# The maxima of a chunk by one product, a third buffer for halves of q and k, and moved slots in an AdaLN block

## The chip, the cores and the metric

The kernel runs on one core of a Trainium2 chip. The metric is the time of one execution in microseconds (us); lower is better. A core has TensorE (PE: matrix products, with its weight loads PEld), VectorE (DVE), ScalarE (ACT), GpSimd (POOL) and SyncE (SP), which here issues nearly all DMA transfers. All data is float32.

## The reference

An AdaLN block: modulated layer norm, causal attention with 16 heads of 16, and a gated feed-forward network with a mix of neighbouring tokens. There are 8 batches of 1024 tokens of 256 numbers. Cut to what is computed:

```python
mod = (silu(c) @ wmod).reshape(8, 6, 1, -1)
sa, ca, ga, sb, cb, gb = (mod[:, 0], ..., mod[:, 5])
ga = (2 * (ga >= 0) - 1) * maximum(abs(ga), 0.25)      # gb in the same way
h = layernorm(x) * (1 + ca) + sa
q, k, v = split(einsum('bnd,ed->bne', h, w_in), 3)      # each as 16 heads of 16
scores = einsum('bhqd,bhkd->bhqk', q, k) * 16 ** -0.5   # causal: -inf above the diagonal
out = softmax(scores) @ v
x = x + ga * (out @ w_out.T + b_out)
h = layernorm(x) * (1 + cb) + sb
xr, xk = mu * h + (1 - mu) * h_prev                     # with mu_r and mu_k
x = x + gb * sigmoid(xr @ W_r.T) * (square(relu(xk @ W_k.T)) @ W_v.T)
```

## The kernel before

**Units and chunks.** A batch has two chunks of 512 tokens (c = 0, 1). Attention is cut into 32 units u: four heads of one batch. A unit's q and k lie on the chip as 128 partitions: four strips of 32 rows, one for each head, of which 16 hold the head's numbers. Row 16 of a strip of q holds the negated maximum of each query, and that of k holds ones, so that the second product of the scores comes out with its maximum subtracted.

**Two passes over the scores.** The first pass ("S") makes scores with queries on the partitions (`pp`, by `maxima`), and VectorE takes their maxima into a small tile `max`; the second ("T") makes them again with keys on the partitions (`pw`, by `weights`), ScalarE takes the exponential into `w`, POOL clears what lies above the diagonal, and `attend` multiplies with v into `po`. A pass goes through a unit in nine pieces: a to e touch the diagonal, 0 to 3 are whole. When all maxima of a chunk are there, `join` (for chunk 1) and, a step later, `subtract` run: products with the identity turn the maxima (`pmx`), ScalarE negates them (`mrow`), and a transfer (`q<-mrow`) writes them into row 16 of the strips of q.

**The loop.** `step` runs once for each number `now`: one piece of T for one unit, one piece of S for a unit that is 9 steps (`LAG`) ahead, both in two halves of two heads, products of both halves first; then what is due in `soon` (subtract among it), then the slot's list `fill`, and last `finish`, which calls `attend` where a group of pieces ends. TensorE, and from the loop on every engine, takes its instructions in the order in which the program gives them (`InOrder`). A function handed to `later` issues its transfer at the start of a later step, urgent ones first; SyncE works through them in order and waits for each one's data.

**Banks.** PSUM has four one-bank buffers with tag "t" (`pw` of the four heads, `pmx`, `po` and all products of the fill, in turn) and two of two banks with tag "s" (`pp`, a half each).

**Slots.** The tables `POST`, `PREP`, `PREP_FIRST`, `START` and others say in which step a piece of other work stands; an entry is a step and a name, entries of one step run in the order of the table. `START` and `compact` count from step 0, the others from step 9 + 36 b, b being the batch whose second pass begins there: this stretch is called a stage below. In `POST` (stages 1 to 6), x and y are the two chunks of the batch before: project (a product py, added to x by VectorE), stats, norm, turn, mix and mixed (VectorE; mixed0 into `mix`, mixed1 into `step`), receptance, key, value (a product pkv, multiplied with r by VectorE, added by POOL). In `PREP` (stages 1 to 6) and `PREP_FIRST` (stage 0), m and n are the two chunks of the next batch: stats, norm, turn (transposes into hT), q0, k0, q1, k1 (a product pq of half the heads, copied by ScalarE to a buffer `qk`, and written to DRAM a step later as `pad<-qk`, from where q and k of a unit are read) and v0, v2 (a product pv, copied to v). `START` does it for batch 0, beside `direct`, which makes q and k of the first units without DRAM; `compact` packs the weights of q and k, which the products pq need.

**Gates.** `gates` runs in step 17: a product, two copies of ScalarE, five operations of POOL, and a transfer of the gates to DRAM.

Every engine instruction is recorded by one helper, so all rows of the profile name its line, L123; they are told apart by their tiles. Instructions of one tile for pieces a to e carry the piece in the name (`pp_a`, `w_a`), whole ones don't.

Of the kernel before, what the change touches and what calls it, by code (L numbers as in the profile page):

```python
# [8 lines left out]
F32 = mybir.dt.float32  # L9
# [5 lines left out]
P = 128  # L15
# [3 lines left out]
CW = 512  # L19
NC = N // CW  # L20
NT = CW // P
HG = 4
# [7 lines left out]
KEPT = 4  # L30
# [42 lines left out]
def adaln_block(  # L73
# [72 lines left out]
    def later(f, steps=1, urgent=False):  # L146

        if strict[0]:
            due.append((clock[0] + steps, not urgent, f))
        else:  # L150
            f()
# [82 lines left out]
    q_of, k_of = [], []  # L234
# [43 lines left out]
    def row_of(t):  # L278

        return strips(t)[:, HD, :]  # L280
# [30 lines left out]
    def gates():  # L311

        pg = bank("pg")
        for c in range(DC):
            pe.matmul(
                pg[:B, :],
                scT[:, c, :],
                wgate[:, c].rearrange("p n e -> p (n e)"),
                start=(c == 0),
                stop=(c == DC - 1),  # L320
            )
        both = sb.tile([B, 2, 2 * D], F32, tag="h", bufs=2, name="gates")
        sign, gate = both[:, 0, :], both[:, 1, :]
        act.activation(gate, pg[:B, :], AF.Abs)
        act.copy(sign, pg[:B, :])
        pool.tensor_scalar(sign, sign, 0.0, 2.0, ALU.is_ge, ALU.mult)
        pool.tensor_scalar_max(gate, gate, 0.25)
        pool.tensor_scalar_add(sign, sign, -1.0)
        pool.tensor_mul(gate, gate, sign)
        pool.tensor_scalar_mul(gate[:, D:], gate[:, D:], 0.5)  # L330
        later(lambda: sync.dma_start(gates_of, gate))

    def rows_of_gates(b):

# [81 lines left out]
    def prep(b, c):  # L416
        S = A[b, c]

        def stats(half):
            statistics(S["xa"], S, f"a{b}_{c}", half)  # L420

        def norm(half):
            normalise(S["xa"], S, f"a{b}_{c}", half)
            if half == 0:
                return
            nxt = b * NC + c + 1
            if 1 < nxt < B * NC:
                later(lambda: load_xa(nxt // NC, nxt % NC))

        def turn():  # L430
            S["hT"] = sb.tile([P, DC, CW], F32, tag="hT", bufs=2, name=f"hT{b}_{c}")
            for d in range(DC):
                name = f"pta{b}_{c}_{d}"
                transposed(S["h"], S["hT"][:, d, :], b, d, SHIFT_A, SCALE_A, name)

        def qk(n, half):

            pq = bank(f"pq{b}_{c}_{n}_{half}")
            at = n * D + half * P
            for d in range(DC):  # L440
                pe.matmul(
                    pq,
                    wqk_sb[:, d, at : at + P],
                    S["hT"][:, d, :],
                    start=(d == 0),
                    stop=(d == DC - 1),
                )
            w = sb.tile([P, CW], F32, tag="qk", bufs=2, name=f"qk{b}_{c}_{n}_{half}")
            if n == 0:
                act.mul(w, pq, SCALE)  # L450
            else:
                act.copy(w, pq)

            later(lambda: sync.dma_start(padded_of[b % 2][n][half][c, :, :HD, :], w))

        def v(t0):
            pv = bank(f"pv{b}_{c}_{t0}")
            rows(pv, S["hT"], wv_sb, (t0, t0 + 1))
            to = v_of[(b * NC + c) % (2 * NC)]
            act.copy(  # L460
                to[:, t0 : t0 + 2, : H * (HD + 1)].rearrange(
                    "p t (h e) -> p t h e", e=HD + 1
                )[:, :, :, :HD],
                pv.rearrange("p (t h e) -> p t h e", t=2, e=HD),
            )

        return dict(
            stats0=lambda: stats(0),
            stats1=lambda: stats(1),
            norm0=lambda: norm(0),  # L470
            norm1=lambda: norm(1),
            turn=turn,
            q0=lambda: qk(0, 0),
            k0=lambda: qk(1, 0),
            q1=lambda: qk(0, 1),
            k1=lambda: qk(1, 1),
            v0=lambda: v(0),
            v2=lambda: v(2),
        )
# [30 lines left out]
    def maxima(u, k, half):  # L510


        V = U[u]
        q, kk = q_of[u % KEPT], k_of[u % KEPT]
        js = (2 * half, 2 * half + 1)
        pp = ps_s.tile([P, 2, CW], F32, tag="s", name=f"pp{u}_{k}_{half}")
        parts, at = [], 0
        for c, i, diagonal in STEPS[k]:
            if ("max", c) not in V:

                V["max", c] = sb.tile(
                    [P, c + 1, HG * NT], F32, tag=f"max{c}", bufs=2, name=f"max{u}_{c}"
                )
            t = NT - 1 - i if diagonal else i
            n = (t + 1) * P if diagonal else CW
            parts.append((c, t, slice(at, at + n), diagonal))
            at += n

        def products(m):
            if m >= len(parts):  # L530
                return
            c, t, cols, diagonal = parts[m]
            q0 = c * CW + t * P
            k0 = c * CW if diagonal else 0
            for n2, j in enumerate(js):
                rs = slice(j * ST, (j + 1) * ST)
                pe.matmul(
                    pp[:, n2, cols],
                    q[rs, q0 : q0 + P],
                    kk[rs, k0 : k0 + cols.stop - cols.start],  # L540
                    start=True,
                    stop=True,
                )

        def largest():
            for c, t, cols, diagonal in parts:
                n = cols.stop - cols.start
                mx = V["max", c][:, 0 if diagonal else 1]
                to = mx[:, t * HG + js[0] : t * HG + js[0] + 2]
                if diagonal:  # L550

                    for n2 in range(2):
                        dve.tensor_tensor_reduce(
                            out=pp[:, n2, cols],
                            in0=pp[:, n2, cols],
                            in1=mask[:, CW - n :],
                            scale=1.0,
                            scalar=-3e38,
                            op0=ALU.add,
                            op1=ALU.max,  # L560
                            accum_out=to[:, n2 : n2 + 1],
                        )
                else:
                    dve.tensor_reduce(to, pp[:, :, cols], AX.X, ALU.max)

        return products, largest
# [7 lines left out]
    def subtract(u, c):  # L574

        V = U[u]
        mx = V["max", c]
        pt = bank(f"pmx{u}_{c}")
        for t in range(NT):
            pe.transpose(  # L580
                pt[:HG, t * P : (t + 1) * P], mx[:, 0, t * HG : (t + 1) * HG], ident
            )
        row = sb.tile([HG, CW], F32, tag="mrow", name=f"mrow{u}_{c}")
        act.mul(row, pt[:HG, :], -1.0)
        later(
            lambda: sync.dma_start(row_of(q_of[u % KEPT])[:, c * CW : (c + 1) * CW], row),
            urgent=True,
        )

# [515 lines left out]

    POST = """
    -12 x.load; -6 x.bias; 6 x.project0; 7 x.stats0; 7 y.load; 8 x.project2; 9 x.stats1; 9 x.norm0;
    10 x.norm1; 10 y.bias; 11 x.turn; 12 x.mix; 13 x.mixed00; 13 x.mixed01; 15 x.mixed10;
    15 y.project0; 16 y.stats0; 17 y.norm0; 17 y.project2; 17 x.mixed11; 18 y.stats1;
    19 x.receptance0; 19 y.norm1; 20 y.turn; 20 x.receptance2; 20 x.key0; 21 y.mix; 22 x.key1;  # L1110
    22 y.mixed00; 22 y.mixed01; 24 x.value0; 24 y.mixed10; 25 y.mixed11; 26 x.value2;
    28 y.receptance0; 29 y.receptance2; 29 y.key0; 31 y.key1; 33 y.value0; 35 y.value2
    """

# [12 lines left out]
    """  # L1127
    GATES = "16 rows; 26 fold0; 34 fold1"
    START = """
    0 n.turn; 4 m.q1; 5 m.k1; 6 n.q1; 7 n.k1; 8 m.v0; 10 m.v2; 11 n.v0; 13 n.v2  # L1130
    """

    PREP_FIRST = """
    6 m.stats0; 7 m.stats1; 8 m.norm0; 9 m.norm1; 10 m.turn; 11 m.q0; 11 n.stats0; 11 m.k0;
    12 n.stats1; 13 n.norm0; 14 n.norm1; 15 n.turn; 15 n.q0; 17 n.k0; 19 m.v0; 20 m.v2; 20 m.q1;
    22 m.k1; 22 n.q1; 24 n.k1; 26 n.v0; 28 n.v2
    """
    END = """
    16 x.load; 18 x.bias; 26 y.load; 28 x.project0; 28 y.bias; 29 x.project2; 30 x.stats0;
# [14 lines left out]
    for n, of in (  # L1154
# [5 lines left out]
        (3, (1, 1, 1)),  # L1160
    ):
        slots[n].append(lambda of=of: direct(*of))
    slots[3].append(lambda: compact())
    for n, m, half in ((1, 0, 1), (4, 1, 0), (6, 1, 1), (8, 0, 0)):
        slots[n].append(lambda m=m, half=half: clear_dram(m, half))
    slots[17].append(gates)
# [47 lines left out]
    def compact():  # L1214
        for c in range(DC):
            act.copy(
                wqk_sb[:, c, :].rearrange("p (h e) -> p h e", e=HD), padded[c][:, :, :HD]
            )
# [95 lines left out]
```

## Time and profile before

| | |
|---|---|
| median of three runs | 1411.76 us (1409.19 to 1415.02) |
| profiled execution, its own time | 1412.37 us |
| its span, first to last instruction | 1410.7 us |
| granted TensorE clock, mean | 0.995 |
| pmx: products, weight loads | 256 and 256; one product 272 ns |
| mrow: negations by ScalarE | 64, 569 ns each |
| q<-mrow: transfers | 64 of 8 KB, issue 546 ns |
| pad<-qk: transfers | 60 of 256 KB |
| maxima of a whole piece, one half (VectorE) | 1219 ns |

A row of a timeline has the start in us, the time in us, the engine, the line, the operation, output and input tiles with their shapes, the count of instructions merged into it, and in brackets the idle time of the engine before it and what ended it. Products of TensorE overlap, so the duration of one is longer than the distance to the next. A steady stage takes 165 us, and its steps repeat to some 0.01 us.

### The profile page before, as it was taken

What the parts mean: (1) busy time and instruction counts of PE and PEld (TensorE: products, weight loads), DVE (VectorE), ACT (ScalarE), POOL (GpSimd) and SP (SyncE); (2) the same over time, 40 slices, a digit from 0 to 9 for tenths busy, and PEclk for the clock granted to TensorE, in tenths of its full rate; (3) what the DMA queues carried; (4) which work ended last, traced back from release to release, by engine and by line L of the source; (5) the groups of instructions that cost most, each with busy time, mean ns of one, the idle gap of its engine ahead of it and who ended that gap; (6) DMA issues with size and microseconds to landing.
All of it is one profiled execution on the core that took longest, in us unless ns stands there. A gap on an engine that the chain in (4) does not pass through costs nothing.

```text
span 1410.7 us, 29817 instructions
## 1 busy us (share of the span) xinstructions
PE 1382.5 (98%) x11285; PEld 758.2 (54%) x11285; DVE 1063.3 (75%) x2872; ACT 894.7 (63%) x1695; POOL 550.9 (39%) x841
## 2 busy tenths in 40 slices
PE   9999999999999999999999999999999999989997
PEld 5544555555555555555554555556555555555545
DVE  6777687788777878788877787778887886878524
ACT  3466666666666666666666666666666666566561
POOL 1142242435423454334534355234643344345431
PEclk9999999999999999999999999999999999999999
DMA  6512423222222323223242222323231232301101
GB/s 192 182 36 79 132 77 114 62 97 82 86 79 77 107 70 106 74 66 106 77 129 57 101 84 66 99 77 107 69 104 56 62 107 71 100 24 37 61 5 34
DMA packets 80816, 118.15 MB, mean 84 GB/s; under 512 B 10136, under 2 KB 38680, under 8 KB 80672
## 3 DMA queue, kind: packets, MB, share of 16 engines
q1 hardware_dynamic: 80336, 115.92, 25.4%
q8 instruction: 89, 1.46, 0.4%
q14 instruction: 55, 0.45, 0.1%
q10 hardware_dynamic: 336, 0.33, 0.1%
HBM read 70.63 MB, written 44.55 MB: 82 GB/s over the span
## 4 chain that ended last, share of the span: by engine, by line
PE 91%; DVE 4%; DMA 2%; ACT 2%; POOL 1%; issue 1%; ACTq 0%; SPq 0%; DVEq 0%; POOLq 0%
PE pw L123 12%; PE po L123 8%; PE pp L123 7%; PE pq L123 7%; PE po_c L123 5%; PE po_e L123 5%; PE pr L123 4%; PE py L123 4%; PE pv L123 4%; PE pkv L123 4%; PE pk L123 4%; PE pw_a L123 3%; PE pw_e L123 3%; PE pw_c L123 2%; PE pmx L123 2%; PE pw_b L123 2%
## 5 line engine op out<-in xcount | busy, mean ns | idle before, releaser
L123 DVE TENSOR_REDUCE max<-pp 128x2 f32<-128x1024 f32 x256 | 302.1, 1219 | 65.3 <-PE pp L123 63.1
L123 ACT ACTIVATE w<-pw 128x512 f32<-128x512 f32 x512 | 265.0, 603 | 83.9 <-PE pp L123 60.6
L123 PE MATMUL pw<-q,k 32*128 32x512 f32 x1024 | 265.6, 617 | 0.7 <-ACT w_i L123 0.6
L123 PE MATMUL pp<-k,q 32*128 32x512 f32 x1024 | 256.0, 620 | 0.0
L123 PEld LDWEIGHTS pw<-q,k 32*128 32x128 f32 x1024 | 108.1, 183 | 100.1 <-issue 58.8
L123 DVE DVE_READ_ACCUMULATOR2_ANT max<- 128x1 f32 x1024 | 144.7, 141 | 0.0
L123 DVE CUSTOM_DVE_ANT_0 pp_c<-pp_c,mask 128x256 f32<-128x256 f32 x240 | 102.3, 436 | 46.2 <-PE pp_c L123 40.1
L123 DVE CUSTOM_DVE_ANT_0 pp_b<-pp_b,mask 128x128 f32<-128x128 f32 x240 | 102.4, 437 | 43.8 <-PE pp_b L123 37.5
L123 DVE CUSTOM_DVE_ANT_0 pp_e<-pp_e,mask 128x512 f32<-128x512 f32 x128 | 88.3, 707 | 55.2 <-PE pp_e L123 52.9
L123 PE MATMUL po<-w,v 128*32 128x512 f32 x1024 | 124.7, 605 | 0.0
L123 DVE CUSTOM_DVE_ANT_0 pp_d<-pp_d,mask 128x128 f32<-128x128 f32 x240 | 102.4, 437 | 28.9 <-PE pp_d L123 22.8
L123 PE MATMUL pq<-hT,wqk_sb 128*128 128x512 f32 x240 | 114.0, 607 | 1.0 <-ACT hT L123 1.0
L123 DVE CUSTOM_DVE_ANT_0 pp_a<-pp_a,mask 128x512 f32<-128x512 f32 x128 | 87.8, 707 | 12.6 <-PE pp_a L123 10.4
L123 POOL TENSOR_TENSOR xb<-xb,r 128x512 f32<-128x512 f32 x30 | 41.7, 1390 | 135.1 <-DVE r L123 110.0
L123 ACT ACTIVATE w_a<-pw_a 128x512 f32<-128x512 f32 x128 | 66.3, 603 | 41.6 <-PE pp_a L123 38.5
L123 POOL TENSOR_TENSOR o<-o,more 128x512 f32<-128x512 f32 x62 | 78.6, 1267 | 33.1 <-ACT more L123 33.0
L123 POOL TENSOR_TENSOR rsb<-rsb,m_half 128x2 f32<-128x2 f32 x30 | 21.4, 714 | 175.3 <-DVE rsb L123 174.0
L123 PEld LDWEIGHTS pp<-k,q 32*128 32x128 f32 x1024 | 82.9, 183 | 4.0 <-DVE max L123 3.6
L123 ACT ACTIVATE w_d<-pw_d 128x512 f32<-128x512 f32 x120 | 63.0, 601 | 21.5 <-PE pp_e L123 19.2
L123 ACT ACTIVATE w_e<-pw_e 128x512 f32<-128x512 f32 x128 | 66.1, 605 | 15.7 <-PE pp_c L123 13.5
L123 ACT ACTIVATE w_b<-pw_b 128x512 f32<-128x512 f32 x120 | 62.1, 603 | 18.2 <-PE pp L123 17.6
L123 ACT ACTIVATE w_c<-pw_c 128x512 f32<-128x512 f32 x120 | 62.2, 603 | 15.3 <-PE pp_b L123 10.8
(212 smaller groups left out, 3034.7 us busy)
## 6 DMA issues: line engine op xcount, KB each, us to landing
pad<-qk SPq DMA_DIRECT2D x60, 256.0 KB
q<-pad SPq DMA_DIRECT2D x30, 512.0 KB
k<-pad SPq DMA_DIRECT2D x30, 512.0 KB
od<-o SPq DMA_DIRECT2D x60, 256.0 KB
xa<-in_x SPq DMA_DIRECT2D x16, 512.0 KB
xb<-in_x SPq DMA_DIRECT2D x16, 512.0 KB
oT<-od SPq DMA_DIRECT2D x60, 128.0 KB
ov<-over SPq DMA_DIRECT2D x30, 256.0 KB
```

Source lines behind the costliest of these rows:

```text
L123: made = f(*args, **kwargs)
```

## The change

`subtract` turns all maxima of a chunk by one product instead of four: VectorE now writes them ordered by head first and tile of tokens second, so that one transpose of 128 x 16 gives 16 partitions of 128, and the transfer to the strips of q takes its 512 numbers of a head from four partitions. The tile `qk` gets three buffers instead of two. The gates' transfer is issued three steps after `gates` instead of one. In the tables, x.mixed10 goes behind y.project0 in step 15 of `POST`, y.mixed01 from step 22 to 24, and x.value0 in step 24 behind the two mixes; m.q1 and m.k1 of `START` go a step ahead, and `compact` too; in `PREP_FIRST` n.q0 goes from 15 to 16, n.v0 from 26 to 29 and n.v2 from 28 to 31. No other arithmetic is changed.

```diff
--- before.py
+++ after.py
@@ -328,7 +328,7 @@
         pool.tensor_scalar_add(sign, sign, -1.0)
         pool.tensor_mul(gate, gate, sign)
         pool.tensor_scalar_mul(gate[:, D:], gate[:, D:], 0.5)
-        later(lambda: sync.dma_start(gates_of, gate))
+        later(lambda: sync.dma_start(gates_of, gate), 3)
 
     def rows_of_gates(b):
 
@@ -445,7 +445,7 @@
                     start=(d == 0),
                     stop=(d == DC - 1),
                 )
-            w = sb.tile([P, CW], F32, tag="qk", bufs=2, name=f"qk{b}_{c}_{n}_{half}")
+            w = sb.tile([P, CW], F32, tag="qk", bufs=3, name=f"qk{b}_{c}_{n}_{half}")
             if n == 0:
                 act.mul(w, pq, SCALE)
             else:
@@ -546,7 +546,7 @@
             for c, t, cols, diagonal in parts:
                 n = cols.stop - cols.start
                 mx = V["max", c][:, 0 if diagonal else 1]
-                to = mx[:, t * HG + js[0] : t * HG + js[0] + 2]
+                to = mx.rearrange("p (j t) -> p j t", t=NT)[:, js[0] : js[0] + 2, t]
                 if diagonal:
 
                     for n2 in range(2):
@@ -576,14 +576,16 @@
         V = U[u]
         mx = V["max", c]
         pt = bank(f"pmx{u}_{c}")
-        for t in range(NT):
-            pe.transpose(
-                pt[:HG, t * P : (t + 1) * P], mx[:, 0, t * HG : (t + 1) * HG], ident
-            )
-        row = sb.tile([HG, CW], F32, tag="mrow", name=f"mrow{u}_{c}")
-        act.mul(row, pt[:HG, :], -1.0)
+
+        pe.transpose(pt[: HG * NT, :P], mx[:, 0], ident)
+        row = sb.tile([HG * NT, P], F32, tag="mrow", name=f"mrow{u}_{c}")
+        act.mul(row, pt[: HG * NT, :P], -1.0)
+        to = row_of(q_of[u % KEPT])[:, c * CW : (c + 1) * CW]
         later(
-            lambda: sync.dma_start(row_of(q_of[u % KEPT])[:, c * CW : (c + 1) * CW], row),
+            lambda: sync.dma_start(
+                to.rearrange("j (t n) -> j t n", t=NT),
+                row,
+            ),
             urgent=True,
         )
 
@@ -1105,10 +1107,10 @@
 
     POST = """
     -12 x.load; -6 x.bias; 6 x.project0; 7 x.stats0; 7 y.load; 8 x.project2; 9 x.stats1; 9 x.norm0;
-    10 x.norm1; 10 y.bias; 11 x.turn; 12 x.mix; 13 x.mixed00; 13 x.mixed01; 15 x.mixed10;
-    15 y.project0; 16 y.stats0; 17 y.norm0; 17 y.project2; 17 x.mixed11; 18 y.stats1;
+    10 x.norm1; 10 y.bias; 11 x.turn; 12 x.mix; 13 x.mixed00; 13 x.mixed01; 15 y.project0;
+    15 x.mixed10; 16 y.stats0; 17 y.norm0; 17 y.project2; 17 x.mixed11; 18 y.stats1;
     19 x.receptance0; 19 y.norm1; 20 y.turn; 20 x.receptance2; 20 x.key0; 21 y.mix; 22 x.key1;
-    22 y.mixed00; 22 y.mixed01; 24 x.value0; 24 y.mixed10; 25 y.mixed11; 26 x.value2;
+    22 y.mixed00; 24 y.mixed01; 24 y.mixed10; 24 x.value0; 25 y.mixed11; 26 x.value2;
     28 y.receptance0; 29 y.receptance2; 29 y.key0; 31 y.key1; 33 y.value0; 35 y.value2
     """
 
@@ -1127,13 +1129,13 @@
     """
     GATES = "16 rows; 26 fold0; 34 fold1"
     START = """
-    0 n.turn; 4 m.q1; 5 m.k1; 6 n.q1; 7 n.k1; 8 m.v0; 10 m.v2; 11 n.v0; 13 n.v2
+    0 n.turn; 3 m.q1; 4 m.k1; 6 n.q1; 7 n.k1; 8 m.v0; 10 m.v2; 11 n.v0; 13 n.v2
     """
 
     PREP_FIRST = """
     6 m.stats0; 7 m.stats1; 8 m.norm0; 9 m.norm1; 10 m.turn; 11 m.q0; 11 n.stats0; 11 m.k0;
-    12 n.stats1; 13 n.norm0; 14 n.norm1; 15 n.turn; 15 n.q0; 17 n.k0; 19 m.v0; 20 m.v2; 20 m.q1;
-    22 m.k1; 22 n.q1; 24 n.k1; 26 n.v0; 28 n.v2
+    12 n.stats1; 13 n.norm0; 14 n.norm1; 15 n.turn; 16 n.q0; 17 n.k0; 19 m.v0; 20 m.v2; 20 m.q1;
+    22 m.k1; 22 n.q1; 24 n.k1; 29 n.v0; 31 n.v2
     """
     END = """
     16 x.load; 18 x.bias; 26 y.load; 28 x.project0; 28 y.bias; 29 x.project2; 30 x.stats0;
@@ -1160,7 +1162,7 @@
         (3, (1, 1, 1)),
     ):
         slots[n].append(lambda of=of: direct(*of))
-    slots[3].append(lambda: compact())
+    slots[2].append(lambda: compact())
     for n, m, half in ((1, 0, 1), (4, 1, 0), (6, 1, 1), (8, 0, 0)):
         slots[n].append(lambda m=m, half=half: clear_dram(m, half))
     slots[17].append(gates)
```

## The prediction

> **What bounds the kernel now.** I read the page first, its busy row and the chain that ended last.
>
> ```profile
> PE 1382.5 (98%) x11285; PEld 758.2 (54%) x11285; DVE 1063.3 (75%) x2872; ACT 894.7 (63%) x1695; POOL 550.9 (39%) x841
> PE 91%; DVE 4%; DMA 2%; ACT 2%; POOL 1%; issue 1%; ACTq 0%; SPq 0%; DVEq 0%; POOLq 0%
> ```
>
> TensorE sets the end: a change is worth the time by which a TensorE start moves. Then I read TensorE's timeline step by step and looked for steps longer than others of their shape. A step's scores take 1.93 to 2.03 us when nothing is late; the places below are those that the change touches and where they take more.
>
> **The product for the maxima.** TensorE's timeline at a last maximum of chunk 1, then ScalarE's in the same stretch:
>
> ```profile
> 418.08 0.60 PE L123 MATMUL pmx<-ident,max 128*4 128x128 f32 x4
> 418.61 1.92 PE L123 MATMUL po<-w,v 128*32 128x512 f32 x16
> ```
>
> ```profile
> 417.75 0.59 ACT L123 ACTIVATE w_a<-pw_a 128x512 f32<-128x512 f32 x1
> 419.18 0.57 ACT L123 ACTIVATE mrow<-pmx 4x512 f32<-4x512 f32 x1
> ```
>
> A product lasts 272 ns, but their starts are 108 ns apart, and the group takes 0.53 us (418.08 to 418.61). Three products less are 3 x 0.108 = 0.32 us of TensorE; for 64 chunks 20.7 us. I don't take that. The banks of PSUM with tag "t" go round in four: the step's four pw take them all, pmx takes the first again, and po the second, which is free only after the second exponential. That one (the row shown) ends at 418.34. A wait of TensorE ends some 0.05 us after its releaser (below: xb ends at 451.38, the load starts at 451.43), so po can start at 418.39 and not at 418.29: 0.22 us gained. Where pmx isn't 0.06 us late, as with 8 of the 26 chunks 1 in full steps, it is 0.16. For chunk 0 (pmx at 400.80, second exponential to 401.16, po_e at 401.33, can start at 401.22) it is 0.11. In all 25 x 0.11 + 18 x 0.22 + 8 x 0.16 = 8.0 us; the other 13 products (start, end, and steps where VectorE holds the scores) could give up to 3.8 us and lie partly beside VectorE's work: half, 1.9. Sum **-9.9**; ends: 0 (all of it taken back by the next wait) and -20.7 (po not held by its bank).
>
> The negation on 16 x 128 instead of 4 x 512 costs between 0.22 us (the page's smallest ScalarE row, 16 columns) and the 0.57 of now; ScalarE is not what po waits for there, since the four exponentials stand ahead of it. I count it as nothing; without cover it would help. The row's transfer becomes 16 pieces of 512 B in place of 4 of 2 KB. It is read first by pw_c at 424.32, 4.6 us after the negation's end (419.74); in the one case where TensorE waited for it, 1.9 us passed from issue to use. That leaves 2.7 us of cover: nothing. VectorE writes its maxima 16 B apart instead of side by side, one or two numbers a partition: nothing, up to the 25% that VectorE is idle.
>
> **Third buffer for halves of q and k.** ScalarE's timeline, then TensorE's:
>
> ```profile
> 431.82 0.59 ACT L123 COPY qk<-pq 128x512 f32<-128x512 f32 x1 [1.99 <-DMA pad<-qk]
> ```
>
> ```profile
> 432.46 0.37 PE L123 MATMUL pw_d<-q,k 32*128 32x128 f32 x1 [0.26 <-ACT qk L123]
> ```
>
> k0 of a batch's second chunk waits for the transfer of k1, two halves before, and pw_d's last bank is k0's. That step's scores take 2.68 us, against 2.03 elsewhere; the six such steps lose 0.62, 0.65, 0.97, 0.63, 0.44 and 0.51. With a third buffer k0 takes one whose transfer was issued seven steps before, and its copy ends at about 431.62, before the bank is asked for (431.71). **-3.8**, ends -3.8 and -1.9. The next half with a new wait would be n.k1, at step 13: its buffer's transfer is issued two steps earlier, and the ones shown take 4.8 us on the chain.
>
> **y.project0 ahead of x.mixed10** (step 15 of a stage, six stages). VectorE, then TensorE's weight loads:
>
> ```profile
> 449.67 0.53 DVE L123 RECIPROCAL few<-few 64x64 f32<-64x64 f32 x1
> 450.13 0.64 DVE L123 SCALAR_TENSOR_TENSOR step<-step,mus,h2T 128x512 f32<-128x512 f32 x1
> 450.70 0.67 DVE L123 TENSOR_TENSOR xb<-xb,py 128x512 f32<-128x512 f32 x1
> ```
>
> ```profile
> 451.43 0.18 PEld L123 LDWEIGHTS pw<-q,k 32*128 32x128 f32 x1 [0.27 <-DVE xb L123]
> ```
>
> py's bank is the fourth pw's of the next step, and its sum stands behind mixed10. These scores take 2.50 us, 0.57 too many. Swapped, the sum starts at 450.13 and frees the bank 0.57 earlier, exactly as needed. 6 x 0.57 = **-3.4**; ends -3.4 and 0.
>
> **y.mixed01 from step 22 to 24, x.value0 behind it and mixed10.** VectorE at step 24:
>
> ```profile
> 488.84 2.35 DVE L123 TENSOR_REDUCE max<-pp 128x2 f32<-128x1024 f32 x2 [0.18 <-PE pp L123]
> 491.80 0.69 DVE L123 SCALAR_TENSOR_TENSOR r<-r,pkv 128x512 f32<-128x512 f32 x1 [0.60 <-PE pkv L123]
> 492.40 0.75 DVE L123 SCALAR_TENSOR_TENSOR step<-step,mus,h2T 128x512 f32<-128x512 f32 x1
> ```
>
> The gain: the scores of step 24 take 2.19 us, since VectorE came late out of step 22 (two mixes of 1.47 and 0.90); 0.26 x 6 = -1.6. The loss: r now runs as soon as pkv is there and frees pkv's bank at 492.5, which the fourth pw of step 25 asks for at 492.55 (0.86 after that step's start at 491.69, as in the step above). After the change two mixes at a spacing of 0.66 stand ahead of r: it runs from 492.43 to 493.12, TensorE goes on at 493.17, and with the 0.26 gone it would have asked at 492.29: 0.88 x 6 = +5.3. Behind r wait POOL's sum into xb and the next maxima; neither was asked for within a step. Together **+3.7**; ends -1.6 and +5.3.
>
> **The gates' transfer, two steps later.** TensorE, SyncE, and the table of windows (us, PE, PEld, DVE, ACT, POOL busy, clock, DMA):
>
> ```profile
> 99.15 0.80 PE L123 MATMUL pw_c<-q,k 32*128 32x256 f32 x2 [1.94 <-DMA q<-mrow]
> ```
>
> ```profile
> 96.84 0.32 SPq L123 DMA_DIRECT2D gates<-gates  x1
> 97.27 0.52 SPq L123 DMA_DIRECT2D q<-mrow  x1
> ```
>
> ```profile
> 99.10:102.40 3.30, 3.25 (x24) 2.39 (x24) 1.44 (x7) 1.08 (x2) 1.51 (x3) 0.51 0.68 232
> ```
>
> POOL ends the gates at 96.82; SyncE waits for that, with the row of maxima behind it, though that was ready at 92. The scores of this step take 6.33 us instead of 1.94, partly since the granted clock falls to 0.51 after the idle time. Past the row, the transfer holds only x's load and one of o for under a microsecond. Some 0.4 us stay: the fourth pw waits for hT, which VectorE ends at 97.36. 6.33 - 2.4, and 0.16 of the products behind (3.69 for 3.53): **-4.1**, ends -2.3 (the wait alone) and -4.5. The Trainium skill ("TensorE: Matmul & The Clock Gate", Part 1: The HAM clock gate) halves the clock only after an idle window of about 3.4 us. Here 1.94 us were enough, so the row decides; by the rule this term would be near -2.3.
>
> **The other slots, all once.** Rows of TensorE:
>
> ```profile
> 123.72 1.98 PE L123 MATMUL pq<-hT,wqk_sb 128*128 128x512 f32 x4 [0.97 <-ACT hT L123]
> ...
> 186.95 0.70 PE L123 MATMUL pp_e<-k,q 32*128 32x512 f32 x2 [0.61 <-DVE max L123]
> ```
>
> n.q0, one step after n.turn, no longer waits for hT (2.07 us of pta instead of 0.93): -1.2, its copy and transfer going a step later too. n.v0 and n.v2, eight products and a copy of ScalarE each, leave steps 26 and 28, where they cost 1.92 each, for 29 and 31. There VectorE's maxima hold the scores: the pairs of steps from 181.60 and from 190.30 take 6.40 and 6.44, 2.4 and 2.6 over their shapes. Walking steps 25 to 32 with two score buffers (VectorE 2.4 us a whole step, 4.2 for b and c) I find 2.8 us of stalls in place of 5.0: -2.2; ends 0 and -3.8. At the start m.q1 (four products, 1.91 us, a copy of 0.6, a transfer) goes into step 3, before pp_e, which takes 2.79 there and 1.07 without a wait; compact's two copies (1.12) find ScalarE idle in step 2. Maxima come 1.2 us later for it, so -1.1; ends 0 and -1.9. Together **-4.5**.
>
> **Sum:** -9.9 - 3.8 - 3.4 + 3.7 - 4.1 - 4.5 = -22.0. The profiled execution took 1412.37 us (span 1410.7), 0.6 above the median of the three runs: 1390.4, as a prediction **1390**, with a range of its own from 1383 to 1397.
>
> **Rivals.** (B) po isn't held by its bank: the load before it waits on ScalarE, but whether for the second exponential the trace can't tell, since pmx covers that time. Then 20.7 in place of 9.9: 1379.6. (C) The mixes cost nothing at step 24, since r isn't last for the bank: -1.6 in place of +3.7: 1385. Against it: the fit to 0.05 us above. (D) TensorE's shorter product is taken back, as the next scores meet VectorE (75% busy, over 80% in some slices) or the copy of po, which ScalarE runs without a gap at 420.63: the first term 0, and 1400. (E) The late things only change names, and the stalls of mixes, buffers and slots return one step on: the gates alone remain, 1408. (F) Slower: the row's 16 pieces land late. From 2.7 us of delay on each chunk 1 would hold pw_c, as at 99.15, where 1.94 us of idle time cost 4.1 with the clock. A delay of 4 us would cost 1.3 us in each of 30 chunks, 39 less the 22: 1429. Against it: 8 KB, as before.
>
> **Numbers.** My forecast 0.50, B 0.12, C 0.13, D 0.15, E 0.06, F 0.04. A measurement of this kernel can tell 0.5%, about 7 us: faster is below 1404.7, so A to D, 0.90; same E, 0.06; slower F, 0.04. The range from 1379 to 1401 takes in B and D.
>
> **What would show it.** The group pmx followed by po 0.3 us after, po starting 0.05 us after the second exponential; no ScalarE wait for pad<-qk; scores of step 16 at 1.93 and of step 25 near 2.8; no TensorE wait for the row near 99 us, with the clock at 1.00; 64 products of 128*16. It is wrong if po follows pmx at 0.2 (B), if step 25 keeps 1.93 (C), or if SyncE's row is what pw_c waits for (F).

## The result, and the profile after

The changed kernel takes 1392.1 us (median of four runs, 1391.8 to 1394.2); the kernel before, run beside it on the same chip, 1411.8 (1409.2 to 1415.0). The ratio is 0.9862 [0.9845, 0.9880]: 17 to 22 us gained, 1390 forecast. The profiled execution has a span of 1392.5 us.

The busy row of the page after and its chain that ended last:

```profile
PE 1362.3 (98%) x11093; PEld 751.1 (54%) x11093; DVE 1061.3 (76%) x2872; ACT 876.1 (63%) x1695; POOL 545.0 (39%) x841
PE 90%; DVE 4%; ACT 3%; POOL 1%; issue 1%; DMA 0%; ACTq 0%; DVEq 0%; POOLq 0%
```

TensorE has 192 products fewer (3 x 64) and still sets the end; the 2% of DMA in the chain are gone.

**The product for the maxima.** TensorE's timeline after, at the last maximum of a chunk 0 and of the chunk 1 behind it (weight loads and products):

```profile
393.26 0.28 PE L123 MATMUL pmx<-ident,max 128*16 128x128 f32 x1
393.74 0.19 PEld L123 LDWEIGHTS po_e<-w_e,v 128*32 128x32 f32 x8 [0.39 <-issue]
393.77 0.64 PE L123 MATMUL po_e<-w_e,v 128*32 128x512 f32 x4 [0.23 <-ACT w L123]
...
410.52 0.28 PE L123 MATMUL pmx<-ident,max 128*16 128x128 f32 x1
410.83 0.16 PEld L123 LDWEIGHTS po<-w,v 128*32 128x32 f32 x8 [0.23 <-ACT w_a L123]
410.84 0.64 PE L123 MATMUL po<-w,v 128*32 128x512 f32 x4
```

ScalarE's timeline after in the same places, and at the copy of k0 in step 12:

```profile
393.04 0.59 ACT L123 ACTIVATE w<-pw 128x512 f32<-128x512 f32 x1
...
410.19 0.59 ACT L123 ACTIVATE w_a<-pw_a 128x512 f32<-128x512 f32 x1
...
411.62 0.25 ACT L123 ACTIVATE mrow<-pmx 16x128 f32<-16x128 f32 x1
...
423.18 0.59 ACT L123 COPY qk<-pq 128x512 f32<-128x512 f32 x1 [1.12 <-PE pq L123]
```

In chunk 1 the second exponential ends at 410.78 and po's load starts at 410.83: the group takes 0.31 us (0.53 before). In chunk 0 it ends at 393.63, but po_e's product starts only at 393.77: 0.51, almost what it was. The negation went from 0.57 to 0.25 us. k0's copy waits for its product only, no more for `pad<-qk`.

**Step 25.** The fourth pw's load, then ScalarE and VectorE ahead of it, after:

```profile
484.05 0.18 PEld L123 LDWEIGHTS pw<-q,k 32*128 32x128 f32 x1 [0.65 <-ACT w L123]
```

```profile
483.40 0.60 ACT L123 ACTIVATE w<-pw 128x512 f32<-128x512 f32 x1 [1.73 <-PE pp L123]
```

```profile
481.92 0.74 DVE L123 SCALAR_TENSOR_TENSOR mix<-step,mus,h2T 128x512 f32<-128x512 f32 x1
482.58 0.75 DVE L123 SCALAR_TENSOR_TENSOR step<-step,mus,h2T 128x512 f32<-128x512 f32 x1
483.25 0.68 DVE L123 SCALAR_TENSOR_TENSOR r<-r,pkv 128x512 f32<-128x512 f32 x1
```

These scores take 2.87 us (482.25 to 485.12) instead of 1.93. Both mixes stand ahead of r, which ends at 483.93. But the load starts 0.05 after ScalarE's first exponential of the same step (to 484.00), not after r. The waits in the compiled programs say why: the banks have changed places.

```
before   pw22_2_3 [waits DVE]           po22_1 [waits Activation]
after    pw22_2_3 [waits Activation]    po22_1 [waits DVE]
```

Before, the fourth pw had pkv's bank and po that of the step's first exponential; after, it is the other way round. The exchange comes and goes with the order of the mixes: experiments 1, 8 and 9 have the waits of before, experiment 3 those of after. The weight load of po in step 25, before and after, shows it too:

```profile
493.62 0.16 PEld L123 LDWEIGHTS po<-w,v 128*32 128x32 f32 x8 [0.76 <-ACT w L123]
...
485.12 0.16 PEld L123 LDWEIGHTS po<-w,v 128*32 128x32 f32 x8 [0.76 <-DVE max L123]
```

**The stretch that the gates held**, in the table of windows (us, PE, PEld, DVE, ACT, POOL busy, clock, DMA share, GB/s):

```profile
99.10:102.40 3.30, 3.30 (x8) 1.36 (x8) 3.16 (x13) 1.68 (x3) 2.92 (x5) 1.00 0.25 84
```

TensorE is busy all through it, at full clock.

**n.q0.** Weight loads after, in the step behind n.turn:

```profile
119.93 0.49 PEld L123 LDWEIGHTS pw<-q,k 32*128 32x128 f32 x2 [0.36 <-ACT hT L123]
120.69 0.18 PEld L123 LDWEIGHTS pw<-q,k 32*128 32x128 f32 x1 [0.27 <-ACT w L123]
```

The wait for hT, which pq had, is now that of the next scores, with a second one for the step's first exponential behind it (2.87 us in place of 1.93).

Measured by the same place in the work, a steady stage takes 163.7 us instead of 165.2.

### The profile page after: what moved, and what is told of

It reads as the page before. It is cut to its first block, busy times and chain, and to the rows that moved or that the text cites. A ratio compares the mean times of both kernels' runs of the same rounds, so it can differ in the third digit from the quotient of the medians.

```text
span 1392.5 us, 29440 instructions
## 1 busy us (share of the span) xinstructions
PE 1362.3 (98%) x11093; PEld 751.1 (54%) x11093; DVE 1061.3 (76%) x2872; ACT 876.1 (63%) x1695; POOL 545.0 (39%) x841
## 4 chain that ended last, share of the span: by engine, by line
PE 90%; DVE 4%; ACT 3%; POOL 1%; issue 1%; DMA 0%; ACTq 0%; DVEq 0%; POOLq 0%
PE pw L123 11%; PE po L123 8%; PE pq L123 8%; PE pp L123 7%; PE po_c L123 5%; PE po_e L123 5%; PE pr L123 4%; PE py L123 4%; PE pv L123 4%; PE pkv L123 4%; PE pk L123 4%; PE pw_a L123 3%; PE pw_e L123 3%; PE pw_c L123 2%; PE pw_b L123 2%; ACT w L123 2%
## 5 line engine op out<-in xcount | busy, mean ns | idle before, releaser
L123 POOL TENSOR_TENSOR xb<-xb,r 128x512 f32<-128x512 f32 x30 | 38.9, 1298 | 141.3 <-DVE r L123 116.2
L123 PEld LDWEIGHTS pq<-hT,wqk_sb 128*128 128x128 f32 x240 | 42.7, 191 | 52.0 <-issue 35.4
```

What stands on the lines that cost most here:

```text
L123: made = f(*args, **kwargs)
```

## The clock between runs

The runs of one kernel differ by up to 11 us, and that hangs on the clock. Each run comes with its mean granted clock. A straight line through all 145 timed runs of the 14 kernels here (one constant for each kernel, one slope for all) has a slope of 1.02 us for each 0.001 of clock (plus or minus 0.07; here and below for 95%) and leaves a scatter of 0.84 us. The differences of the constants compare kernels at equal clock; what a change does to the clock itself is then left out of them and stands in the plain times. Both are in this table; the ratio is to the kernel before, on the same chip, and the clock is the mean over the kernel's runs.

```
kernel                                   median   ratio [95%]              clock    equal clock: to before, to after (+-)
before (60 runs)                           -      1                        0.9964      0
after                                    1392.1   0.9862 [0.9845, 0.9880]  0.9980    -16.7    0
mixes as before                          1391.5   0.9865 [0.9848, 0.9883]  0.9952    -20.9   -4.2 (1.2)
START, compact as before                 1392.9   0.9881 [0.9864, 0.9898]  0.9970    -16.9   -0.1 (1.1)
product behind po                        1386.4   0.9835 [0.9817, 0.9853]  0.9952    -25.3   -8.6 (1.1)
product behind po, r ahead of the mixes  1381.5   0.9789 [0.9765, 0.9813]  0.9994    -25.9   -9.1 (1.1)
product behind po, mixes as before       1380.9   0.9791 [0.9772, 0.9809]  0.9986    -27.8  -11.1 (1.1)
n.q0, n.v0, n.v2 as before               1399.1   0.9918 [0.9902, 0.9933]  0.9940    -14.7    2.0 (1.1)
n.v0, n.v2 as before                     1397.5   0.9892 [0.9872, 0.9912]  0.9946    -16.0    0.7 (1.1)
n.q0 as before                           1393.6   0.9877 [0.9857, 0.9898]  0.9965    -16.9   -0.2 (1.2)
before with the product alone            1405.6   0.9963 [0.9949, 0.9978]  0.9957     -6.6 (0.7)
before with the gates' move alone        1407.8   0.9980 [0.9963, 0.9996]  0.9967     -2.1 (0.5)
before with the third buffer alone       1406.4   0.9968 [0.9952, 0.9984]  0.9953     -5.1 (0.5)
before with y.project0 first alone       1406.5   0.9969 [0.9953, 0.9985]  0.9969     -3.1 (0.5)
```

## The experiments

**1. The mixes back.** In the changed kernel, the diff's line of `POST` for steps 22 to 26 undone.

```diff
-    22 y.mixed00; 24 y.mixed01; 24 y.mixed10; 24 x.value0; 25 y.mixed11; 26 x.value2;
+    22 y.mixed00; 22 y.mixed01; 24 x.value0; 24 y.mixed10; 25 y.mixed11; 26 x.value2;
```

> The changed kernel with y.mixed01 back in step 22 and x.value0 ahead of y.mixed10. Theory (r behind two mixes holds pkv's bank, which step 25 asks for): step 25's scores go from 2.87 us to 1.93, step 24's from 1.93 to 2.19, six times each, so 6 x (0.94 - 0.26) = 4.1 us less, 1388.0. Rival (the move is free, the 2.87 comes from something else): 2.87 stays and the time rises by the 1.6 that the move gained, 1393.7.

1391.5 us, so by the plain times almost nothing. But the profile has a stage of 163.0 us instead of 163.7, with step 25's scores back at 1.93 and step 24's at 2.21, and also this (table of windows):

```profile
1327.60:1337.80 10.20, 10.11 (x41) 4.47 (x40) 3.34 (x5) 3.91 (x7) 2.19 (x4) 0.50 0.05 11
```

Ten microseconds at half clock near the end took most of the lead back: 7.1 us over the changed kernel at the last unit's first weights, 2.9 at the end. At equal clock the old order is 4.2 us better, the six stages of 0.7. So this part of the change is a loss, of the size forecast (3.7).

**2. START and compact back.**

```diff
-    0 n.turn; 3 m.q1; 4 m.k1; 6 n.q1; 7 n.k1; 8 m.v0; 10 m.v2; 11 n.v0; 13 n.v2
+    0 n.turn; 4 m.q1; 5 m.k1; 6 n.q1; 7 n.k1; 8 m.v0; 10 m.v2; 11 n.v0; 13 n.v2
...
-    slots[2].append(lambda: compact())
+    slots[3].append(lambda: compact())
```

> The changed kernel with m.q1, m.k1 and compact back in their old steps. Theory (moved ahead they leave step 5 without a product, TensorE works too thinly there and its granted clock falls, 0.57 from 43 to 47 us): the clock stays at 1.00 there, the product pq of step 6 takes 1.91 instead of 3.37, the first pw_a starts near 51.5 and not at 53.09, 1390.5. Rival (the fall of the clock is by chance and the earlier start is a gain of 1.1, as predicted): a fall shows here too or not at all in a second run, and the time is 1392 to 1393.3.

The theory that this move caused the fall of the clock at 43 us falls: it fell here too, at 36.3. 1392.9 us, 0.1 below the changed kernel at equal clock (plus or minus 1.1), where the prediction had a loss of 1.1. The profiles without a fall in the first 85 us reach unit 1's first weights at 87.7 to 88.4 us with the new slots and at 88.2 to 88.8 with the old, on average 0.3 apart: next to nothing.

**3. The product behind po.** In the changed kernel, `subtract` is kept back until `finish` has issued the step's po, so that po takes the bank that the product took, free after the first exponential.

```diff
-                    soon.append((now + 1, lambda c=c: subtract(u, c)))
+                    soon.append((now + 1, lambda c=c: turns.append(lambda: subtract(u, c))))
...
             finish(T1, now)
+        while turns:
+            turns.pop(0)()
```

> The changed kernel with the product for the maxima placed behind po instead of ahead of it, where both fall into one step. Theory (po waits for the second of four banks, that is for the second exponential): po now takes the first bank and starts 0.01 us after the scores, the product behind it costs 0.2, so a group is 0.2 us beyond po: 0.30 less for each of 25 chunks 0, 0.11 to 0.16 less for each of 26 chunks 1, some 10.5 us, 1381.6. Rival (what po waits for isn't its bank, or the row comes too late when turned 1.9 us later): no gain, 1392, or pw_c waits for the row.

TensorE's timeline of this kernel:

```profile
406.98 0.64 PE L123 MATMUL pw_a<-q,k 32*128 32x512 f32 x2
...
407.56 1.92 PE L123 MATMUL po<-w,v 128*32 128x512 f32 x16
409.42 0.28 PE L123 MATMUL pmx<-ident,max 128*16 128x128 f32 x1
409.62 0.38 PE L123 MATMUL pw_b<-q,k 32*128 32x128 f32 x2
```

po follows the scores without a wait, the product 1.86 behind it, and the scores 0.20 behind that, in chunk 0 as well. In the compiled program po now waits for the first exponential instead of the second. The stage takes 162.26 us, 1.45 less; 8.6 in all at equal clock, where 10.5 was forecast. (The median of 1386.4 is 4.8 above the forecast; 2.9 of that goes with the clock, 0.9952 in place of 0.9980.) The row of maxima, turned later, now holds TensorE in two places, 0.4 us at 60.6 us and 0.9 near the end. This shows that the second exponential's bank was what held po, and what of the 20.7 was left lying there.

**4. The product alone**, on the kernel before: its order of maxima, the one product and the transfer.

```diff
-                to = mx[:, t * HG + js[0] : t * HG + js[0] + 2]
+                to = mx.rearrange("p (j t) -> p j t", t=NT)[:, js[0] : js[0] + 2, t]
...
+        pe.transpose(pt[: HG * NT, :P], mx[:, 0], ident)
```

> The kernel before with the one product, its order of maxima and its transfer alone. Theory: 0.02 us for each of 25 chunks 0 and 0.16 to 0.22 for each of 26 chunks 1 (5.8 us), and up to 3 us from the other 13, so 1403 to 1406. Rival (no bank holds po): 20.7 us, 1391. Rival (ScalarE's shorter negation gives the time): more than 9 us.

5.2 us by the ratio, 6.6 at equal clock. The groups have the lengths of the changed kernel (0.51 and 0.31). Six steps 12 take 17.3 us here and 16.0 in the kernel before: with two buffers, 1.3 of the gain goes to the wait for `pad<-qk`.

**5 to 7. Three other parts alone**, each on the kernel before.

```diff
-        later(lambda: sync.dma_start(gates_of, gate))
+        later(lambda: sync.dma_start(gates_of, gate), 3)
```

> The kernel before with the gates' transfer two steps later and nothing else. Theory: no TensorE wait for the row of maxima near 99 us, granted clock 1.00 there, the scores of that step near 2.4 instead of 6.33, 4.1 us less (ratio 0.997). Rival (the clock falls there for another reason): 2.3 us less and a fall of the clock within the same 10 us.

The table of windows of this kernel:

```profile
99.10:102.40 3.30, 3.30 (x16) 1.35 (x18) 3.10 (x13) 1.36 (x4) 1.98 (x4) 1.00 0.31 88
...
183.20:186.60 3.40, 3.40 (x20) 0.59 (x16) 2.54 (x8) 1.92 (x5) 1.33 (x3) 0.51 0.06 19
```

The wait and the fall at 99 us are gone (scores 2.38 instead of 6.33), and by 113 us the profile is 4.0 ahead as forecast. Falls at 183 and 193 us (10.24 us at half clock in all) took 4.9 of it back in this execution, by unit 4's first weights. By the medians of that chip (1411.6 before) 3.9 are left, by the ratio 2.8 (0.6 to 5.2), at equal clock 2.1: the wait alone, without its fall.

```diff
-            w = sb.tile([P, CW], F32, tag="qk", bufs=2, name=f"qk{b}_{c}_{n}_{half}")
+            w = sb.tile([P, CW], F32, tag="qk", bufs=3, name=f"qk{b}_{c}_{n}_{half}")
```

> The kernel before with the third buffer for halves of q and k and nothing else. Theory: ScalarE waits for pad<-qk nowhere, the scores of step 12 take 2.03 in all six stages, 3.8 us less (ratio 0.9973). Rival (pw_d's bank is held by the copy anyway): the ScalarE wait goes and 0.3 us or more of each step's loss stays.

5.1 at equal clock. ScalarE of this kernel in step 12, where the row before had 1.99 of wait for the transfer:

```profile
430.37 0.59 ACT L123 COPY qk<-pq 128x512 f32<-128x512 f32 x1 [1.12 <-PE pq L123]
```

None of the six steps is long any more, and no other took their place. The same step of stage 0 goes from 2.31 to 2.03 as well, so the rows give 4.1; the other 1.0 of the 5.1 is not traced.

```diff
-    10 x.norm1; 10 y.bias; 11 x.turn; 12 x.mix; 13 x.mixed00; 13 x.mixed01; 15 x.mixed10;
-    15 y.project0; 16 y.stats0; 17 y.norm0; 17 y.project2; 17 x.mixed11; 18 y.stats1;
+    10 x.norm1; 10 y.bias; 11 x.turn; 12 x.mix; 13 x.mixed00; 13 x.mixed01; 15 y.project0;
+    15 x.mixed10; 16 y.stats0; 17 y.norm0; 17 y.project2; 17 x.mixed11; 18 y.stats1;
```

> The kernel before with y.project0 ahead of x.mixed10 in step 15 and nothing else. Theory: the scores of step 16 take 1.93 instead of 2.50 in six stages, 3.4 us less (ratio 0.9976), and no other scores take longer. Rival: mixed10, now behind the sum, holds the maxima of step 16, and step 17 loses what step 16 gains.

3.1 at equal clock. Step 16's scores go from 450.28 to 452.20, 1.92 us, in every stage; the step behind it is no longer.

**8. The product behind po, and r ahead of both mixes.** The edits of experiment 3, and:

```diff
-    22 y.mixed00; 24 y.mixed01; 24 y.mixed10; 24 x.value0; 25 y.mixed11; 26 x.value2;
+    22 y.mixed00; 24 x.value0; 24 y.mixed01; 24 y.mixed10; 25 y.mixed11; 26 x.value2;
```

> The changed kernel with the product for the maxima behind po, and with x.value0 in step 24 ahead of y.mixed01 and y.mixed10. Theory: the 0.94 us of step 25 goes and step 24 keeps 1.93, 6 x 0.94 = 5.7 us less than with po first alone (ratio 0.9835 to the kernel before, 0.4% less: 0.9795, some 1380.5 where the kernel before takes 1409.3); scores of steps 24 and 25 both at 1.93. Rival (VectorE is merely late one step on): the maxima of step 25 start 0.7 us late behind the mixes and hold the scores of step 26; 2 us or less are gained.

The rival came true. Weight loads of this kernel, one step later than the old wait:

```profile
482.85 0.30 PEld L123 LDWEIGHTS pp<-k,q 32*128 32x128 f32 x4 [0.26 <-DVE max L123]
```

Step 25 is back at 1.93, but with two mixes behind r VectorE's next maxima are late, and step 26's scores take 2.75. The stage is 162.1, 0.1 less than in experiment 3, and at equal clock the difference is 0.6 plus or minus 1.1. That the median is 5 us better is the clock's: 0.9994 against 0.9952. So it is luck that 1381.5 comes near the theory's 1380.5.

**9. The product behind po, and the mixes as before.** The edits of experiments 3 and 1 together.

> The changed kernel with the product for the maxima behind po and with the mixes of steps 22 and 24 as before the change. Theory: the two gains add up, since the stall that the order with value0 ahead of both mixes left in step 26 (0.82) is not there with mixed01 back in step 22: a stage of 161.5 to 161.6 us (162.2 with the product behind po alone, less 0.7), step 25's scores 1.93 and step 26's near 2.0; the whole some 4 us below the version with the product behind po alone, 1380 to 1383. Rival: here too the stall only moves on, to another step of 24 to 27, and the stage stays at 162.1 to 162.2, the whole at 1384 to 1387.

1380.9 us, the ratio 0.9791 [0.9772, 0.9809]. The total is where the theory put it, but the stage takes 161.8, not 161.5. Weight loads of this kernel in steps 23 and 24:

```profile
471.88 0.44 PEld L123 LDWEIGHTS po_e<-w_e,v 128*32 128x32 f32 x8 [0.56 <-POOL w_e L123]
...
475.21 0.62 PEld L123 LDWEIGHTS pw<-q,k 32*128 32x128 f32 x4 [0.24 <-ACT o L123]
475.83 0.30 PEld L123 LDWEIGHTS pp<-k,q 32*128 32x128 f32 x4
```

Step 25's 0.94 is gone, 0.30 is back in step 24, and po_e, now 0.26 late, waits for POOL's mask of w_e: 0.4 a stage is left of the 0.7. It beats the changed kernel by 11 us, and at equal clock the version of experiment 8 by 2.0 plus or minus 1.0.

**10. n.q0, n.v0 and n.v2 back.**

```diff
-    12 n.stats1; 13 n.norm0; 14 n.norm1; 15 n.turn; 16 n.q0; 17 n.k0; 19 m.v0; 20 m.v2; 20 m.q1;
-    22 m.k1; 22 n.q1; 24 n.k1; 29 n.v0; 31 n.v2
+    12 n.stats1; 13 n.norm0; 14 n.norm1; 15 n.turn; 15 n.q0; 17 n.k0; 19 m.v0; 20 m.v2; 20 m.q1;
+    22 m.k1; 22 n.q1; 24 n.k1; 26 n.v0; 28 n.v2
```

> The changed kernel with n.q0, n.v0 and n.v2 of the first stage back in steps 15, 26 and 28. Prediction's terms: 1.2 and 2.2 lost again, so 3.4 more, 1395.5, of which 1.2 by the time of the scores near 130 us. Theory from the trace after: n.q0 is worth 0.1 only (its wait for hT went into the next scores, 0.94), n.v0 and n.v2 1.6: 1.7 more, 1393.8; in the profile the first weights of units 1 to 2 come 0.1 apart from the changed kernel's, those of units 2 to 4 some 1.6.

1399.1 us, 7 more than the changed kernel and past both numbers. At equal clock it is 2.0, near the theory's 1.7; the rest goes with the clock, 0.9940 in place of 0.9980. So I took the two moves apart.

**11. n.v0 and n.v2 back, n.q0 left.** The second line of the diff above alone.

> The changed kernel with n.v0 and n.v2 of the first stage back in steps 26 and 28, n.q0 left in step 16. Theory: this alone is behind the loss of the version with all three back; the two stretches in which VectorE's maxima hold the scores come back near 180 and 190 us, some 2 us in the profile by unit 3 and again a clock of 0.5 between 175 and 200, which no profile with the new slots has: 1396 to 1400. Rival: the loss of that version is falls of the clock that happen to any kernel, and the slots are worth the 1.6 of the trace: 1392 to 1395, no fall at 175 to 200.

1397.5 us. The table of windows of this kernel, two windows of 3.41 us, and the second of them after the change:

```profile
179.09:182.50 3.41, 2.35 (x20) 1.28 (x16) 3.24 (x15) 1.98 (x5) 1.99 (x5) 1.00 0.88 313
182.50:185.91 3.41, 3.26 (x16) 0.91 (x20) 2.61 (x9) 1.59 (x5) 0.64 (x1) 0.50 0.08 32
```

```profile
182.50:185.91 3.41, 3.41 (x50) 1.99 (x52) 1.74 (x6) 2.64 (x5) 2.09 (x5) 1.00 0.00 0
```

VectorE's maxima hold the scores, TensorE is busy for 2.35 us of a window, and the clock is at half for the next. From unit 2's first weights to unit 4's it is 2.6 us more than in the changed kernel (76.45 and 73.85); that fall explains 1.7 at most. Without a fall there, the kernel before and experiments 6 and 7, which have the old slots and four products, take 75.5 to 75.8: 1.9 more at most. Four of the seven profiles with these slots as before show falls between 175 and 200 us (experiments 4, 5, 10 and 11; the kernel before and experiments 6 and 7 not), and none of the seven with the new ones. At equal clock only 0.7 plus or minus 1.1 is left: what the two moves bring they bring mostly through the clock. The theory's total holds; how much of the 5.4 is the move's and how much falls elsewhere stays open, since the mean clock is that of five runs.

**12. n.q0 back alone.** The first line.

> The changed kernel with n.q0 of the first stage back in step 15, n.v0 and n.v2 left in 29 and 31. Prediction's term: 1.2 lost, 1393.3. Theory from the trace after: 0.1 lost, since hT only holds the next scores instead (0.94 there): within 2 us of the changed kernel, and its first weights of unit 2 at the same distance from those of unit 1 to 0.2 us.

1393.6 us; from unit 1's first weights to unit 2's 40.4 us against 40.3. TensorE's timeline of this kernel:

```profile
117.86 1.09 PE L123 MATMUL pta<-ident,ha 128*128 128x128 f32 x8
119.93 1.98 PE L123 MATMUL pq<-hT,wqk_sb 128*128 128x512 f32 x4 [0.97 <-ACT hT L123]
```

Here pq waits for hT by 0.97 and the next scores don't wait at all; after the change pq doesn't wait, and the scores do by 0.94. The forecast 1.2 was no gain.

## Why the prediction was right, point by point

The number was right, and the mechanism of most terms. A term alone against its measurement (at equal clock where a run isolates it):

**Product, -9.9: mis-sized.** From the start of pmx to the next product, the 64 groups take 33.4 us in all before and 23.6 after: 0.5 less for the 25 chunks 0 (2.75 forecast), 5.2 for the 26 chunks 1 (as forecast) and 4.2 for the other 13 (3.8 at most forecast, and half of it counted). How much of the 4.2 lies beside VectorE's work no run isolates. Alone the product measured -6.6, with 1.3 more given to the buffers; those 7.9 would leave some 2 of the 4.2. The step that failed is "For chunk 0 ... it is 0.11". po_e starts 0.14 behind the second exponential, not 0.05. Its first load needs two things, the exponential and POOL's mask (the compiled program has both waits there, and one alone at po of chunk 1), and the trace has an instruction of TensorE's queue ahead of that load that only waits (51 ns, from 393.67, 0.04 behind the exponential); the load follows at 393.74. So 25 x 0.02 instead of 25 x 0.11. That two waits cost this is read from the trace; no run takes one away. Chunk 1 came as worked out, 0.22 and 0.16, and rival B (po not held by its bank) is ruled out by these rows and by experiment 3. Rival D is true in part: experiment 4 shows 1.3 taken back, by the wait for the buffers and not by VectorE; the third buffer takes that wait away.

**Third buffer, -3.8; y.project0 first, -3.4: right,** the buffer 1.3 too small. Alone they measured -5.1 and -3.1 (plus or minus 0.5), and the stalls went from steps 12 and 16 without coming up elsewhere, which was rival E.

**Mixes, +3.7: right in size by luck, with another releaser.** Step 25 lost 0.94 a stage (forecast 0.88) and step 24 gained 0.26; undoing it brought 4.2. The step "it runs from 492.43 to 493.12, TensorE goes on at 493.17" held for r, but not for TensorE: it waits for the first exponential, which ends 0.07 after r, since the banks of the fourth pw and of po were exchanged. By r alone it would have been 483.98 instead of 484.05, and the loss 0.87. But that exponential ends 1.75 after the step's start (482.25), whatever r does, so with this bank the loss is 0.94 even for an early r. The step that failed is that the fourth pw asks for pkv's bank: the forecast took the dealing of the banks as fixed. Rival C had it right that r is not what the bank waits for, but the loss is there, so C is out.

**Gates, -4.1: right in the profile**, 4.0 by 113 us. The forecast weighed a rule against the row. The Trainium skill ("TensorE: Matmul & The Clock Gate", Part 1: The HAM clock gate) has the clock halve after an idle window of about 3.4 us. By that rule the term would be near -2.3. The trace decides against it as to the fall: in the kernel before and in experiments 4, 6 and 7 the clock halves between 99.2 and 99.9 us, after 1.94 to 2.12 us of idle, in every profile that has the wait and in none without it.

**Other slots, -4.5: too much.** n.q0 -1.2 is near 0 (0.1 in the trace), since hT is only late for the next instruction; START and compact -1.1 is near 0; n.v0 and n.v2 -2.2 measured 0.7 to 5.4, by the clock. The failed step is to price a moved wait as gone without asking which instruction next needs the late thing.

**The transfer in 16 pieces** cost nothing that shows: nowhere in the profile after does a TensorE instruction wait for the row, so rival F is out.

The parts measured at equal clock (product 6.6 and the 1.3, buffer 3.8 by its six steps, sum 3.1, gates 2.1, n.v 0.7, less mixes 4.2) come to 13.4 of the 16.7. The 3.3 left are not traced. Of the other 3 in the plain 19.7 some 1.6 go with the clock (0.9980 in the four runs after, 0.9964 over all runs of the kernel before, times 1.02 us for 0.001); the rest is no more than four runs beside four can leave. Predicted terms erred both ways, and that the sum came out closer than its parts is luck.

## What to carry to other kernels

A shorter chain in front of a wait gains only up to what releases that wait, so look at what holds the next instruction and move it into the gap as well: putting po ahead of the product gained more (8.6 us) than making one product of four (6.6). When a step is moved off a late input, find the next instruction that needs that input or the bank behind it; here that decided n.q0 and the mixes. The trace before could not show it for the mixes, since the move itself exchanged the banks; the compiled program did. Where the times of a kernel differ from run to run, compare at equal granted clock and read each step in the profile before a small change is called a gain or nothing.

## What the hardware showed that was not expected

**The clock falls in windows of 3.413 us.** In each of the 14 profiles the times between falls and rises are whole multiples of 3.413, and a fall lasts 3.413, 6.83 or 10.24 (but for the last of each profile, which is cut off at the end). The mean clock of a run goes with its time at 1.02 us for each 0.001, and one such window at half clock is 0.0012 of the span, so it costs an estimated 1.3 us by the slope and 1.7 at most, half its length. The Trainium skill ("TensorE: Matmul & The Clock Gate", Part 1: The HAM clock gate) gives a free-running window of 3413 ns and two levels, full and half. The traces agree: they have no level but 1.0 and 0.5, and the first window starts anywhere from 0.05 to 3.20 us behind the first instruction. Two kernels with almost the same program and the same phase of these windows to the first scores, experiments 10 and 11 (1.14 and 1.15 us), both show falls at 165.0, 1216.3, 1322.1 and 1363.1 us behind the first scores. With other phases they fall elsewhere, or not at all before the last half microsecond (experiment 8). That the phase decides is suggested by this pair and not shown: experiment 9, 0.05 us from experiment 8 in phase, has one fall more, and no run set the phase alone. A full idle window is not needed: before the fall in experiment 11 TensorE was busy for 2.35 of 3.41 us, and before one in each of experiments 2, 4 and 5 (at 1343.6, 195.2 and 193.5 us) for the whole window, as the profile models it. Nor is busy time the whole rule, since windows with 1.4 to 2.0 us of it were followed by none; what is counted stays open.
